# A graph network kernel: SyncE fetches the last chunk of some units row by row

## The chip, the cores and the metric

The kernel runs on one core of one Trainium2 chip. The core has five instruction streams: TensorE (PE, with its weight loads shown apart as PEld), VectorE (DVE), ScalarE (ACT), GpSimd (POOL) and SyncE (SP). SP computes nothing here: it issues transfers between HBM and the core's memory, one after the other in the order of the program. POOL issues the indirect transfers, whose row numbers come from a tile. The transfers of both run on the same 16 DMA engines.

The metric is the device time of one execution in microseconds, taken as the median of the runs.

## The reference

Four graph layers over 12,500 nodes of 128 features and 212,500 edges, which are sorted by their destination `dst`. Each layer takes a normalised and rectified copy of the node features, does something with the rows of each edge's source, and adds the result to the features:

```python
h = maximum(layernorm(x), 0); x = x + gat2(relu(gat1(h)))     # two graph attention convolutions
h = maximum(layernorm(x), 0); x = x + transformer(h)          # 8 heads, q of the node, k and v of the source
h = maximum(layernorm(x), 0); x = x + message_max(h)          # maximum over a node's edges, then an MLP
h = maximum(layernorm(x), 0)
sums = segment_sum(h[src], dst); x = x + sums / maximum(count(dst), 1)
```

All five edge steps (two in the first layer) need `table[src]`: for each edge one row of a table that was computed per node. This fetching of rows is what the change is about.

## The kernel before

**Tiles, chunks and units.** Nodes are handled in T = 98 tiles of P = 128. Edges are handled in 1661 chunks of 128, one edge to a partition. A unit `u` is U = 17 chunks in a row, which hold nearly all edges of node tile `u`; a tile also looks at the last 3 chunks of the unit before it and at the first 3 of the unit after it, 23 in all. The 17 chunks of a unit are fetched in 6 groups of GS = 3 chunks; the last group has only 2 (chunks 15 and 16).

**Preparation.** `prepared` (L413) derives from the edge lists what the passes need. `sd` holds all source numbers as float, edge after edge along each partition. `chunks(IDX, sd, ...)` (L470) transposes it on PE and DVE writes it as integers into `IDX`, where column k is chunk k. `ch` (L472) is a scratch tile of the same shape as `sd`.

**Five passes.** `edge_pass` (L1321) runs five times: `gat1` over the table `t1` (66 floats a row), `gat2` over `t2` (130), `attn` over `tkv` (264), `max` over `ts_` (128) and `sum` over `th` (129). The classes `gat`, `attn`, `maximum` and `total` say what each pass does with a chunk; `total` is the last one.

**Gathers.** `Pass.gather` (L1230) takes a tile `g` for a group from a ring of `bufs` buffers (18 groups in both gat passes, 17 in attn, 20 in max, 24 in sum) and has POOL issue one indirect transfer for each chunk (L1235): the column of `IDX` names 128 rows of the table, and each row lands in one partition. That makes 8305 gathers in the whole kernel, 1661 a pass.

**Use of a group.** `e1` is the first work on a group. In the gat passes it copies a logit out of `g` on ACT (L1523), in attn it multiplies by the queries on DVE (L1641), in max it transposes `g` on PE (L1701), in sum it does nothing but note where the chunk lies. Later `batch` (L1263) multiplies one-hot matrices (`se`, loaded at L1252, turned into float at L1281 on ACT) with the chunks on PE (L1290) and so sums the edges of a node tile into `acc` in PSUM, four chunks at a time. `ends` (L1294) loads `gt` (L1297, rows for tiles that don't fit the window), copies `acc` to `r` on ACT (L1311), lets DVE pick between `r` and `gt` (L1305) and hands `r` to the pass's own last step. In the sum pass that step is `after_sum`: three small DVE operations up to `o` (L932) and the store of the result by SP (L934).

**Order.** The order of all instructions is written out by hand. `edge_pass` keeps a calendar of rounds, RU = 24 to a unit; each piece of work is a generator that starts in a given round and goes one step further in each round. Within a round, pieces go by rank, lower first. `gather(u, i)` stands in round 24u - 24 + 4i, one unit ahead of `e1(u, i)` in round 24u + 4i. Each engine then works through its own instructions strictly in this order, and so does SP: a store that waits for its data holds up every transfer behind it. SP's transfers take turns over eight semaphores, so each also waits for the eighth before it to land.

Of the kernel before, what the change touches and what calls it, by code (L numbers as in the profile page):

```python
# [65 lines left out]
def gnn_kernel(ctx, tc, a, out):  # L66
# [18 lines left out]
    ww_d = dram.tile([3, D], BF16, name="ww_d")  # L85
    feat_d = dram.tile([T, 5, EW], BF16, name="feat_d")
    last_d = dram.tile([T, 5, EW], BF16, name="last_d")
    ewf_d = dram.tile([3, CP * P], BF16, name="ewf_d")
    first_d = dram.tile([1, (CP + 16) * P], BF16, name="first_d")
    xd = dram.tile([NP, D], F32, name="xd")  # L90
# [194 lines left out]
    def chunks(out, x, on):  # L285

        o = out.rearrange("p (r b) -> p r b", b=RC)
        for b0 in range(0, RC, 4):
            n = min(4, RC - b0)
            px = psum([P, 4, P], "b", "px")  # L290
            for b in range(n):
                PE.transpose(px[:, b, :], x[:, (b0 + b) * P:(b0 + b + 1) * P], ident)
            yield
            on(o[:, :, b0:b0 + n].rearrange("p r b -> p b r"), px[:, :n, :])
# [118 lines left out]
    def prepared(wp):  # L413
        tn_i = wp.tile([P, 1], I32, name="tn_i")
        GP.iota(tn_i, pattern=[[0, 1]], base=0, channel_multiplier=P)
        tid = wp.tile([T, 1], I32, name="tid")
        GP.iota(tid, pattern=[[0, 1]], base=0, channel_multiplier=1)
        tn = wp.tile([P, 1], F32, name="tn")
        V.tensor_copy(tn, tn_i)
        tn1 = wp.tile([P, 1], F32, name="tn1")  # L420
        V.tensor_scalar_mul(tn1, tn, -1.0)
        tn2 = wp.tile([P, 1], F32, name="tn2")
        V.tensor_scalar_add(tn2, tn, float(P))
        yield

        w = rd_[:, 1:EW + 1]
        eq = wp.tile([T, EW - P], BF16, name="eq")  # L430
        long_ = wp.tile([T, 1], F32, name="long_")
        V.scalar_tensor_tensor(eq, w[:, P:], 0.0, w[:, :EW - P], op0=ALU.add, op1=ALU.is_equal,
                               accum_out=long_)
        yield
        f = wp.tile([T, 2], F32, name="f")
        V.tensor_scalar(f[:, 0:1], rd_[:, 0:1], tn[:T, :], long_, op0=ALU.is_ge, op1=ALU.max)
        V.tensor_scalar(f[:, 1:2], rd_[:, EW + 1:], tn2[:T, :], f[:, 0:1], op0=ALU.is_lt,
                        op1=ALU.max)
        V.tensor_scalar_min(f[:, 1:2], f[:, 1:2], 1.0)
        yield  # L440
        p2 = psum([P, P], "mm", "p2")
        PE.transpose(p2[:1, :T], f[:, 1:2], ident[:T, :T])
        yield
        flag = wp.tile([1, T], F32, name="flag")
        V.tensor_copy(flag, p2[:1, :T])
        zr = wp.tile([1, T], F32, name="zr")
        V.memset(zr, 0.0)
        ord_ = wp.tile([1, T], F32, name="ord_")
        V.tensor_tensor_scan(ord_, flag, zr, 0.0, op0=ALU.add, op1=ALU.add)
        V.tensor_copy(NOV, ord_[:, T - 1:T])  # L450

        at = wp.tile([1, T], F32, name="at")
        V.scalar_tensor_tensor(at, flag, -float(2 * T), ord_, op0=ALU.mult, op1=ALU.add)
        V.tensor_scalar_add(at, at, float(2 * T - 1))
        yield
        pfl = psum([P, P], "mm", "pfl")
        PE.matmul(pfl[:, :T], ones[0:1, :], flag, start=True, stop=True)
        p3 = psum([P, P], "mm", "p3")
        PE.transpose(p3[:T, 0:1], at, ident[0:1, 0:1])
        yield  # L460
        V.tensor_copy(FLAG, pfl[:, :T])
        at_i = wp.tile([T, 1], I32, name="at_i")
        V.tensor_copy(at_i, p3[:T, 0:1])
        GP.indirect_dma_start(out=list_d, in_=tid, in_offset=None,
                              out_offset=bass.IndirectOffsetOnAxis(ap=at_i[:, 0:1], axis=0),
                              bounds_check=T - 1, oob_is_err=False)
        SY.dma_start(LIST, list_d.rearrange("(p t) c -> p (t c)", p=1))
        yield

        yield from chunks(IDX, sd, V.tensor_copy)  # L470

        ch = wp.tile([P, RC * P], F32, name="ch")  # L472
        V.tensor_tensor(ch, dd[:, 1:], dd[:, :RC * P], ALU.not_equal)
        yield
        yield from chunks(FIRST, ch, S.copy)
        m = wp.tile([P, RC * P], BF16, name="m")
        S.mul(m, ch, -BIG)
        SY.dma_start(first_d[0, P:(CP + 1) * P].rearrange("(p f) -> p f", p=P), m)
        yield
        dl = w  # L480
        V.tensor_scalar(dl, w, tn1[:T, :], FAR, op0=ALU.add, op1=ALU.min)
        V.tensor_scalar_max(dl, dl, -1.0)
        yield
        xb = wp.tile([T, EW], BF16, name="xb")
        S.copy(xb, dl)
        SY.dma_start(feat_d[:, 2, :], xb)
        hi, lo = yield from square(wp, dl, [T, EW], "q")
        for k, y in ((3, hi), (4, lo)):
            SY.dma_start(feat_d[:, k, :], y)
        yield  # L490
# [700 lines left out]
    def zero_rows(pool):  # L1191
# [3 lines left out]
        for _ in zeroed(gen_d, z, 7):  # L1195
            for _ in range(2 * RU):
                yield

    class Pass:


# [10 lines left out]

        made, whole = True, True

        def __init__(self):
            self.rhs, self.gs, self.f, self.fa, self.x, self.n0 = {}, {}, {}, {}, {}, {}
            self.st, self.se, self.acc = {}, {}, {}

# [6 lines left out]
        def x_load(self, t):  # L1225
            if self.source is not None:
                self.x[t] = features(self.source, t, self.width)
            yield

        def gather(self, u, i):  # L1230
            c, n = groups_of(u)[i]
            g = self.pool.tile([P, GS, self.wid], self.dt, name="g", bufs=self.bufs)
            for j in range(n):
                k = u * U + c + j
                GP.indirect_dma_start(  # L1235
                    out=g[:, j, :], out_offset=None, in_=self.table,
                    in_offset=bass.IndirectOffsetOnAxis(ap=IDX[:, k:k + 1], axis=0))
            self.gs[u, i] = g
            yield
# [81 lines left out]
    def edge_pass(name, table, wid, dt, wids, work_of, post, extra=()):  # L1321
        nonlocal ps_now
        w = work_of
        with tc.tile_pool(name=name, bufs=2) as pool, \
                tc.tile_pool(name="ps_" + name, bufs=1, space=PSUM) as pp, tc.manual_schedule():
            ps_now, w.pool, w.table, w.wid, w.dt, w.wids = (pp, w.banks), pool, table, wid, dt, wids
            cal = {}

            def at(r, rank, g):
                cal.setdefault(r, []).append((rank, g))  # L1330

            for u in range(T):
                r0 = u * RU
                at(r0 - RU, 0, w.load(u))
                at(r0 + RU - 4 - w.tail[0] * (u == T - 1), 0, w.load2(u))
                for i, _ in enumerate(groups_of(u)):
                    at(r0 - RU + i * RG, 0, w.gather(u, i))
                    at(r0 + i * RG, 5, w.e1(u, i))
                    if w.e2_at is not None:
                        e2_at = w.e2_at if u < T - 2 else w.e2_last or w.e2_at  # L1340
                        at(r0 + e2_at[i] - w.tail[0] * (u == T - 1), 4, w.e2(u, i))
                if w.chain_at is not None:
                    at(r0 + w.chain_at - w.tail[0] * (u == T - 1), 3, w.chain(u))
                n = len(w.batches(u))
                rt = r0 + w.tile_at
                loads = rt - RU
                rt -= w.tail[1] * (u == T - 2) + w.tail[2] * (u == T - 1)
                at(min(loads, rt + RU - 9 - 3 * (n - 1) - 2), 0, w.tile_load(u))
                at(rt, 0, w.x_load(u))
                for b in range(n):  # L1350
                    at(rt + RU - 9 - 3 * (n - 1 - b), 2, w.batch(u, b, n))
                at(rt + RU - 4, 1, w.ends(u, post))
            for g in extra:
                at(0, 1, g(pool))
            live, r = [], min(cal)
            while live or cal:
                live += cal.pop(r, [])
                live.sort(key=lambda g: g[0])
                live = [g for g in live if next(g[1], live) is not live]
                r += 1  # L1360
# [116 lines left out]
        V.tensor_tensor(c, x, b, ALU.subtract)  # L1477

    class gat(Pass):
        chain_at, e2_at, tile_at = RU + 5, range(RU + 13, 2 * RU + 1, 2), 2 * RU  # L1480

        def __init__(self, c, source=None):
# [116 lines left out]
            return r  # L1599

    class attn(Pass):
        bufs, source, width = 17, x2d, 2 * D
        chain_at, tile_at = RU + 7, 2 * RU + 2
        e2_at = [RU + 15 + r for r in (0, 2, 4, 6, 7, 11)]
# [68 lines left out]
            return r  # L1673

    class maximum(Pass):
        feats, bufs, source, made = last_d, 20, xd, False
        tile_at, tail = 12, (0, 0, 8)
        banks = {"pm": 1, "x": 2, "acc": 1, "pg": 2, "mm": 2}
# [45 lines left out]
            return r  # L1724

    class total(maximum):
        bufs, made = 24, True
        tile_at, tail = 10, (0, 0, 0)
        banks = {"acc": 2, "mm": 2}
# [173 lines left out]
```

## Time and profile before

| what | value |
|---|---|
| median of 3 runs | 10796.18 us (10791.58 to 10797.74) |
| the profiled execution, its own time | 10805.76 us |
| its span, first to last instruction | 10804.1 us |
| mean granted TensorE clock | 0.721 |
| gathers, first to last, gat1 | 159.7 to 2276.5 us |
| gat2 | 2319.9 to 4401.5 us |
| attn | 4441.5 to 6563.1 us |
| max | 6619.2 to 8694.3 us |
| sum | 8718.3 to 10797.0 us |

The busy share of each engine over the span, in 40 slices of 270 us (a digit is tenths; PEclk is the clock that TensorE was granted, DMA the share of the 16 transfer engines):

```profile
PE   3676666656556556677777777888888866666666
DVE  4555555544444444577777774333333310000000
ACT  4666666644444444355555554444344421111111
POOL 3777777767777777677777776777777767777777
PEclk6555555556676676799999998898888865555555
DMA  4332222224444444455555553333333323333333
```

The five passes can be told apart by the steps in these rows: gat1 up to the ninth digit, gat2 up to the sixteenth or seventeenth, attn to the twenty-fourth, max to the thirty-second, sum to the end. POOL's row hardly changes from pass to pass; the other engines' rows do.

### The profile page before, as it was taken

The numbers are of one execution on the slowest core, as the hardware profiler recorded it, in microseconds if no ns is written. First come the engines' busy times: TensorE is split into PE (matmuls) and PEld (weight loads), VectorE is DVE, ScalarE is ACT, GpSimd is POOL, SyncE is SP. The second block draws the span as 40 slices with busy tenths as digits, with TensorE's granted clock in tenths as the row PEclk, the third lists the DMA queues.
The fourth block names the chain that finished last, engine by engine and source line by source line (L and its number), as shares of the span: only waits on it lengthen the run. The fifth ranks groups of instructions, "written<-read, shape, count | busy, mean of one in ns | idle before, by whom it ended". The sixth has DMA issues, their size and how long they took to land. (4 is left out here: it accounts for less than half of the span.)

```text
span 10804.1 us, 149842 instructions
## 1 busy us (share of the span) xinstructions
PE 7525.6 (70%) x47184; PEld 5611.8 (52%) x47185; DVE 4565.5 (42%) x15188; ACT 4673.1 (43%) x13171; POOL 7928.6 (73%) x8330
## 2 busy tenths in 40 slices
PE   3676666656556556677777777888888866666666
PEld 2333333334444444566666666666666644444444
DVE  4555555544444444577777774333333310000000
ACT  4666666644444444355555554444344421111111
POOL 3777777767777777677777776777777767777777
PEclk6555555556676676799999998898888865555555
DMA  4332222224444444455555553333333323333333
GB/s 127 86 85 74 74 72 73 74 79 118 117 114 117 117 115 117 129 164 167 163 167 162 166 163 102 96 96 96 93 96 96 93 77 81 80 80 81 81 79 78
DMA packets 759391, 1146.93 MB, mean 106 GB/s; under 512 B 224152, under 2 KB 491623, under 8 KB 758479
## 3 DMA queue, kind: packets, MB, share of 16 engines
q0 software_dynamic: 292368, 610.29, 22.7%
q1 hardware_dynamic: 465536, 526.83, 15.0%
q8 instruction: 374, 6.13, 0.2%
q14 instruction: 441, 3.61, 0.1%
q10 hardware_dynamic: 672, 0.07, 0.0%
HBM read 964.76 MB, written 171.69 MB: 105 GB/s over the span
## 5 line engine op out<-in xcount | busy, mean ns | idle before, releaser
L1235 POOL DMA_INDIRECT g<-t,IDX x3322 | 3158.5, 951 | 1171.1 <-issue 692.6
L1290 PE MATMUL acc<-xf,sef 128*128 128x131 f32 (+2 forms) x13458 | 2292.1, 321 | 571.5 <-ACT sef L1281 545.2
L1290 PEld LDWEIGHTS acc<-xf,sef 128*128 128x128 f32 x13458 | 1985.4, 223 | 745.6 <-ACT sef L1281 609.0
L1235 POOL DMA_INDIRECT g<-tkv,IDX x1661 | 1615.8, 973 | 545.8 <-issue 407.4
L1235 POOL DMA_INDIRECT g<-ts__84,IDX x1661 | 1569.4, 945 | 561.8 <-issue 359.5
L1235 POOL DMA_INDIRECT g<-th,IDX x1661 | 1573.0, 947 | 529.6 <-issue 406.0
L1290 PE MATMUL acc<-g,sef 128*128 128x129 f32 x4486 | 1365.3, 445 | 722.2 <-DMA g<-th,IDX 613.2
L1290 PEld LDWEIGHTS acc<-g,sef 128*128 128x128 f32 x4486 | 999.2, 302 | 1088.4 <-DMA g<-th,IDX 732.4
L1281 ACT CAST sef<-se 128x512 f32<-128x512 fp8e4 (+1 forms) x1755 | 1028.6, 598 | 435.7 <-PE acc L1290 430.6
L1305 DVE COPY_PREDICATED r<-FLAG,gt 128x129 f32<-128x129 int32 (+2 forms) x490 | 145.5, 297 | 2139.0 <-ACT r L1311 2077.1
L1706 DVE TENSOR_TENSOR_SCAN fm<-n,fm,pg 128x384 f32<-128x384 bf16 (+1 forms) x585 | 566.3, 968 | 932.8 <-PE pg L1703 931.5
L1518 PE MATMUL ex<-ADX,st 128*128 128x6 bf16 x4486 | 354.4, 174 | 830.3 <-ACT st L1124 373.3
L1518 PEld LDWEIGHTS <-st 128*128 128x128 fp8e4 x4486 | 329.4, 113 | 1000.2 <-ACT st L1124 565.0
L1523 ACT COPY lg<-g 128x3 f32<-128x3 f32 (+1 forms) x1172 | 226.5, 193 | 1150.1 <-DMA g<-t,IDX 1091.3
L1311 ACT COPY r<-acc 128x129 f32<-128x129 f32 (+2 forms) x392 | 105.8, 270 | 1311.9 <-PE acc L1290 1311.8
L1290 PE MATMUL acc<-xs,se 128*128 128x201 bf16 x2243 | 483.7, 368 | 231.2 <-ACT x L1576 120.0
L1716 ACT COPY xf<-pt_f 128x384 f32<-128x384 f32 x586 | 270.5, 462 | 864.8 <-PE pt_f L1712 859.5
L1139 PE MATMUL pm_se<-NF,fa 5*128 5x128 bf16 x4486 | 586.3, 266 | 0.0
L1441 DVE TENSOR_TENSOR_SCAN fw<-n,lt 17x384 f32<-17x384 bf16 (+1 forms) x294 | 303.3, 1032 | 542.3 <-PE lt L1453 542.3
L1124 ACT ACTIVATE st<-pm_st,ones 128x384 fp8e4<-128x384 f32 (+2 forms) x877 | 471.2, 537 | 120.6 <-PE pm_st L1131 120.6
L1636 PE MATMUL qe<-q,st 128*128 128x128 bf16 x6729 | 484.7, 223 | 25.7 <-DVE g L1641 18.4
L1712 PE MATMUL pt_f<-ident,fm 128*128 128x128 f32 x1661 | 340.7, 316 | 208.6 <-DVE xf L1715 142.7
(1099 smaller groups left out, 12341.0 us busy)
## 6 DMA issues: line engine op xcount, KB each, us to landing
se<-se_d SPq DMA_DIRECT2D x294, 368.0 KB
st<-st_d SPq DMA_DIRECT2D x196, 368.0 KB
g<-t,IDX POOLq DMA_INDIRECT x3322
n<-first_d SPq DMA_DIRECT2D x97, 544.0 KB
st_d<-st SPq DMA_DIRECT2D x98, 368.0 KB
se_d<-se SPq DMA_DIRECT2D x98, 368.0 KB
g<-tkv,IDX POOLq DMA_INDIRECT x1661
g<-ts__84,IDX POOLq DMA_INDIRECT x1661
```

What stands on the lines that cost most here:

```text
L1124: S.activation(out, pm[:, :out.shape[1], :], AF.Relu, scale=-1.0, bias=ones[:, 0:1], saturate=False)
L1139: PE.matmul(pm[:, j, :], f[:, (c + j) * P:(c + j + 1) * P], NF, start=True, stop=True)
L1235: GP.indirect_dma_start(out=g[:, j, :], out_offset=None, in_=self.table, in_offset=bass.IndirectOffsetOnAxis(ap=IDX[:, k:k + 1], axis=0))
L1281: S.copy(se, self.se[t][:, at, :])
L1290: PE.matmul(acc[:, :m], se[:, j, :], x[:, i, :], start=(b == 0 and j == 0), stop=(b == n - 1 and j == len(ws) - 1))
L1441: V.tensor_tensor_scan(fw[:, s0 * P:(s0 + n) * P], n0[:, s0 * P:(s0 + n) * P], lt[:r, :n, :].rearrange("p j e -> p (j e)"), fw[:, s0 * P - ...
L1518: PE.matmul(ex[:, 6 * k:6 * k + 6], st, ADX[:, t, :, :].rearrange("p s v -> p (s v)"), start=(first and c0 == 0), stop=(stop and c0 + n - ...
L1523: S.copy(lg[:, 0, 1 + c0:1 + c0 + n, :], self.gs[u, i][:, :n, c + 1:c + 2])
L1636: PE.matmul(qe[0][:, k - c0, :], st, self.q[t][:, s * D:(s + 1) * D], start=(first and s == 0), stop=(stop and s == 2))
L1706: V.tensor_tensor_scan(fm[:, :m, :].rearrange("p j e -> p (j e)"), self.n0[u][:, cols], pg, self.prev, op0=ALU.add, op1=ALU.max)
L1712: PE.transpose(pt[:, j, :], fm[:, j, :], ident)
L1716: S.copy(ft[:, :m, :D], pt[:, :m, :])
```

## The change

It has four parts.

1. The preparation writes the source numbers to HBM a second time, as integers in the order of the edges: DVE copies `sd` into `ch`, SP stores it to `src_x`. `ch` is allocated earlier for it and is written again later, as before.
2. `row_units` picks the units whose last chunk is to be fetched by SP: `by_row = 8` in `gat`, `attn` and `maximum`, that is units 7, 15, ... 95 (12 in each of the four passes); `by_row = 4` in `total`, units 3, 7, ... 95 (24).
3. `fetch_rows(u, span)` is a new piece of work with rank -1, ahead of all else in its rounds. Its 188 rounds (92 in the sum pass) end in round 24u + 12. SP loads the chunk's 128 row numbers into a tile of one partition; then, spread over these rounds, it loads 16 of them at a time into 16 registers and issues one transfer for each row, from `table[v]` to partition q of the tile `gx`. `gx` holds two chunks and has two buffers. That is 9216 rows in the whole kernel.
4. `gather` of such a unit's last group uses `gx` in place of `g`, and POOL fetches only its first chunk. All later work finds the chunk where it found it before.

```diff
+    src_x = dram.tile([CP * P, 1], I32, name="src_x")
...
+        ch = wp.tile([P, RC * P], F32, name="ch")
+        V.tensor_copy(ch.bitcast(I32), sd)
+        SY.dma_start(flat(src_x), ch.bitcast(I32))
+        yield
         yield from chunks(IDX, sd, V.tensor_copy)
 
-        ch = wp.tile([P, RC * P], F32, name="ch")
         V.tensor_tensor(ch, dd[:, 1:], dd[:, :RC * P], ALU.not_equal)
...
+    RR = 16
+    row_regs = [SY.alloc_register(f"row{i}") for i in range(RR)]
...
+        by_row = None
...
+        def row_units(self):
+            if self.by_row is None:
+                return [], 0
+            span = self.by_row * RU - 4
+            return [(u, RU // 2 - span) for u in range(T - 1) if u % self.by_row == self.by_row - 1
+                    and u * RU + RU // 2 - span >= -RU], span
+
+        def fetch_rows(self, u, span):
+            g = self.gx[u] = self.pool.tile([P, 2, self.wid], self.dt, name="gx", bufs=2)
+            rw = self.pool.tile([1, P], I32, name="rw", bufs=2)
+            e0 = (u * U + U - 1) * P
+            SY.dma_start(rw, src_x[e0:e0 + P, :].rearrange("(o f) c -> o (f c)", o=1))
+            for r in range(4):
+                yield
+            q = 0
+            for r in range(span - 4):
+                while q < P and q * (span - 4) < (r + 1) * P:
+                    if q % RR == 0:
+                        SY.load(row_regs, rw[0:1, q:q + RR])
+                    v = SY.snap(row_regs[q % RR], min_val=0, max_val=NP - 1)
+                    SY.dma_start(g[q:q + 1, 1, :], self.table[ds(v, 1), :])
+                    q += 1
+                yield
+
         def gather(self, u, i):
             c, n = groups_of(u)[i]
-            g = self.pool.tile([P, GS, self.wid], self.dt, name="g", bufs=self.bufs)
+            by_row = i == NG - 1 and u in self.gx
+            if by_row:
+                g, n = self.gx.pop(u), n - 1
+            else:
+                g = self.pool.tile([P, GS, self.wid], self.dt, name="g", bufs=self.bufs)
             for j in range(n):
                 k = u * U + c + j
                 GP.indirect_dma_start(
...
+            units, span = w.row_units()
+            for u, r in units:
+                at(u * RU + r, -1, w.fetch_rows(u, span))
...
     class gat(Pass):
+        by_row = 8
     class attn(Pass):
+        by_row = 8
     class maximum(Pass):
+        by_row = 8
     class total(maximum):
+        by_row = 4
```

More of the change, by code (lines that the diff above doesn't have):

```diff
@@ L1213, in gnn_kernel @@
         made, whole = True, True
+        by_row = None
         def __init__(self):
+            self.gx = {}
             self.rhs, self.gs, self.f, self.fa, self.x, self.n0 = {}, {}, {}, {}, {}, {}
```

## The prediction

> **What bounds the kernel now.** I read the share of busy time first, then the costliest groups, then the gathers pass by pass.
>
> ```profile
> PE 7525.6 (70%) x47184; PEld 5611.8 (52%) x47185; DVE 4565.5 (42%) x15188; ACT 4673.1 (43%) x13171; POOL 7928.6 (73%) x8330
> L1235 POOL DMA_INDIRECT g<-t,IDX x3322 | 3158.5, 951 | 1171.1 <-issue 692.6
> L1235 POOL DMA_INDIRECT g<-tkv,IDX x1661 | 1615.8, 973 | 545.8 <-issue 407.4
> L1235 POOL DMA_INDIRECT g<-ts__84,IDX x1661 | 1569.4, 945 | 561.8 <-issue 359.5
> L1235 POOL DMA_INDIRECT g<-th,IDX x1661 | 1573.0, 947 | 529.6 <-issue 406.0
> ```
>
> POOL is busy for only 73%, but the 27% is mostly a gap of its own making: 0.30 us after every gather. The gathers alone, in a window around each pass (start:end, length, busy time and count, then clock, DMA share, GB/s):
>
> ```profile
> 159.00:2277.00 2118.00, 1582.64 (x1661) 0.50 0.30 77
> 2319.00:4402.00 2083.00, 1575.91 (x1661) 0.69 0.40 116
> 4441.00:6564.00 2123.00, 1615.81 (x1661) 0.96 0.56 164
> 6619.00:8695.00 2076.00, 1569.40 (x1661) 0.89 0.33 95
> 8718.00:10804.00 2086.00, 1573.03 (x1661) 0.57 0.31 80
> ```
>
> Length by 1661 gives 1.275, 1.254, 1.278, 1.250 and 1.256 us for a gather, in five passes with quite different clocks and other work. So POOL's rate of issue sets the length of all five. A unit of 17 gathers lasts 17 x 1.25 = 21.25 us. The timeline in the last pass shows it, and SP beside it:
>
> ```profile
> 9618.22 0.95 POOL L1235 DMA_INDIRECT g<-th,IDX  x1 [0.30 <-issue]
> 9619.21 0.31 DVE L1305 COPY_PREDICATED r<-FLAG,gt 128x129 f32<-128x129 int32 x1 [21.30 <-ACT r L1311]
> 9619.47 0.94 POOL L1235 DMA_INDIRECT g<-th,IDX  x1 [0.30 <-DMA g<-th,IDX]
> 9620.32 0.34 SPq L934 DMA_DIRECT2D out_x<-o  x1
> 9620.70 0.43 SPq L727 DMA_DIRECT2D x<-xd  x1
> 9621.23 0.38 SPq L1252 DMA_DIRECT2D se<-se_d  x1
> 9621.65 0.43 SPq L1297 DMA_DIRECT2D gt<-gen_d  x1
> 9640.46 0.34 SPq L934 DMA_DIRECT2D out_x<-o  x1
> ```
>
> Gathers start 1.25 us apart; SP issues four transfers in 1.8 us and then stands at the next store. SP's own waits say the same (total, times, longest):
>
> ```profile
> SPq L934 <- DVE o L932: 1898.8, 98, 27.5
> ```
>
> So 1899 of the last pass's 2086 us of SP are free, and the change spends them.
>
> **What goes.** Units 7, 15, ... 95 (12 of them) lose one gather in each of the first four passes, units 3, 7, ... 95 (24) in the last: 72 of 8305. At 1.25 us, and 1.278 in the attention pass, that is 60 x 1.25 + 12 x 1.278 = 90.3 us, all of it on the path. The two-chunk tile gx adds waits on POOL: in the changed order its gather names eight SP transfer semaphores, but they are those of the rows written to that buffer two row units before, and the sequencer passes such waits while the gather before still runs (every gap is 0.30 us, with such a wait or without). Nothing.
>
> **What comes, on SP.** 9216 rows. In the changed order each is a register operation and a one-row transfer; 16 rows share one load of registers. Rows of before that are nearest:
>
> ```profile
> L958 SPq TENSOR_LOAD <-NOV x4: 271/274/453, 169.3 to 171.6; - x4
> L958 SPq FUSED_REGOPS  x4: 147/147/159, 169.8 to 171.9; - x4
> L467 SPq DMA_DIRECT2D LIST<-list_d x1: 246/246/246, 73.0 to 73.0; - x1
> L603 SPq DMA_DIRECT2D wwr<-in_L_gnn_Wm x1: 291/291/291, 43.0 to 43.0; - x1
> ```
>
> Between two SP instructions lie 0.04 to 0.05 us (9620.66 to 9620.70). So a row, c, costs 0.147 + 0.045 + 0.246 + 0.045 = 0.48 us, and with the slower of each 0.159 + 0.05 + 0.291 + 0.05 = 0.55. No row of before has its address from a register. From below c can't be under 0.45 (0.147, 0.09 and the cheapest store of one row, 0.21); from above the issue of a 128-row load, 0.43, gives 0.72 with 0.16 and two gaps of 0.065. I take 0.52: the mean of 0.48 and 0.55, since a one-row transfer is what it is nearest to; 0.45 and 0.72 stay as ends.
>
> [...]
>
> *Last pass.* In four units POOL now needs 67 x 1.25 = 83.75 us (85 before). SP needs 128 c for rows, 8 x 0.32 = 2.6 for register loads, 2.3 for fetching the indices and waiting for them to land (0.29 and about 2: bounded by 0 and the 3.6 us that the chain of waits shows for a whole gather), and 4 x 1.8 = 7.2 for its transfers of before. With c = 0.52: 66.6 + 12.1 = 78.7. It fits, with 5 us to spare; it is full at c = (83.75 - 12.1)/128 = 0.56. Queued behind rows now are gt (L1297), x and se: some 32 rows, 17 us, push gt from 19 us before its use (9621.65 to 9640) to about 2.6 us before the store, and it has to land within that. If it is 2 us late each unit, DVE and then the store behind it wait, and SP loses 8 us in four units: full at 0.50. I take no loss, as DVE has 21 us idle there and the sums' banks are freed by ACT, not by DVE.
>
> *Other passes.* Eight units are 169 us; SP needs 66.6 + 4.9 + 8 x 12 issues x 0.45 = 115. It is full only at c = 0.94. The last row goes out 9 of a unit's 24 rounds (8 us) before the group's first use, against some 0.5 + 3 us for issue and landing; gather buffers for 17 groups or more take up a slip of a few us before POOL sees it. The cover that hides the rows is SP's free time; gone, each us of SP is a us of the pass.
>
> *Preparation.* DVE copies 128x1664 once more (1.8 us, as L473, 1.87) and a later write of ch waits for its store: 2 us, between 0 and 5.
>
> **Sum.** -90.3 + 2 = -88.3. The profiled execution took 10805.76 us (span 10804.1), 9.6 over the median of the runs shown, 10796.18. So 10717.5 for it and 10708 for the median.
>
> **Rivals.**
> 1. *SP bounds the last pass* (the slower side). From c = 0.56 each four units last 128 c + 12.1, so against before 24 x (128 c + 12.1 - 85) - 58.3: nothing at c = 0.589, over 0.2% slower from 0.596; 10954 us at 0.64, 11200 at 0.72. For it: a new kind of address, and a margin of 0.04 us. Against: four priced parts that all lie below.
> 2. *Rows or gt land too late in passes 1 to 3*, where a group's buffer is held nearly three units: compute slips, POOL waits for a buffer, and the 36 saved gathers come back, 45.3 us: 10753. Against: 8 us of room.
> 3. *Gathers get dearer*, as they share the transfer engines with 9216 rows (the attention pass, at a share of 0.56, has 1.278 for 1.250): 0.005 us each is 41 us, 10749. Against: rows of 0.3 to 1 KB add 9216 packets to 759391.
>
> **How the numbers follow.** A measurement tells 0.2% (21.6 us) from no change. Forecast, 10700 to 10735: 0.55. Rivals 2 and 3, or c of 0.56 to 0.58: 0.12, still faster. Near nothing (c about 0.58 to 0.596): 0.08. Rival 1 beyond: 0.25. So faster 0.67, same 0.08, slower 0.25. The range goes from 10698 (no loss in preparation, and the runs' spread) up to c = 0.62, 10890; beyond lie some 0.15. The likeliest's own range is 10700 to 10735.
>
> **What would show it.** Right: 8233 gathers still 1.25 us apart, SP rows spaced 0.5 to 0.55 us, the last pass's gathers over in about 2049 us, SP still waiting at L934's store. Wrong: rows 0.6 us apart or more, no wait at that store, POOL waiting for PE in the last pass; or a gather gap over 0.30 elsewhere.

## The result

| kernel | median (lowest to highest) | against the kernel before |
|---|---|---|
| before, run beside it | 10797.74 us (10791.58 to 10802.74) | |
| changed | 10915.97 us (10912.67 to 10918.39) | 1.0109 [1.0098, 1.012] |

The change costs 118 us, where a gain of 88 was forecast. Its profiled execution has a span of 10916.7 us, 112.6 more than the one before, at the same mean clock of 0.72.

From the page of the changed kernel, its shares of busy time and POOL's groups of gathers (busy us, mean ns of one, then the idle time ahead of them and what ended most of it):

```profile
PE 7564.5 (69%) x47184; PEld 5666.0 (52%) x47185; DVE 4567.8 (42%) x15189; ACT 4651.3 (43%) x13171; POOL 7854.9 (72%) x8258
L1277 POOL DMA_INDIRECT g<-t,IDX x3274 | 3124.2, 954 | 1179.4 <-issue 647.8
L1277 POOL DMA_INDIRECT g<-tkv,IDX x1637 | 1578.6, 964 | 696.0 <-issue 394.7
L1277 POOL DMA_INDIRECT g<-ts__85,IDX x1637 | 1546.2, 945 | 577.8 <-issue 362.1
L1277 POOL DMA_INDIRECT g<-th,IDX x1613 | 1525.8, 946 | 518.6 <-issue 400.5
```

A gather costs POOL about what it did (954, 964, 945 and 946 ns for 951, 973, 945 and 947), and POOL has 72 instructions and 73.7 us of work fewer. What grew most is one idle time: ahead of the gathers from `tkv`, the attention pass's table, 696.0 us where it was 545.8. The windows around the gathers of each pass of the changed kernel (start:end, length, POOL's busy time and count, granted clock, DMA share, GB/s) give the rest:

```profile
162.00:2280.00 2118.00, 1575.13 (x1649) 0.50 0.29 77
2332.00:4407.00 2075.00, 1571.68 (x1649) 0.70 0.41 116
4447.00:6696.00 2249.00, 1589.92 (x1649) 0.93 0.53 154
6774.00:8835.00 2061.00, 1557.59 (x1649) 0.89 0.33 96
8861.00:10910.00 2049.00, 1548.45 (x1637) 0.57 0.31 82
```

With first starts and last ends to a tenth of a us, and the gap to the next pass's first gather beside them, the 112.6 us fall into place:

| stretch | its gathers, before | after | gap behind it, before | after | change | forecast |
|---|---|---|---|---|---|---|
| up to the first gather | | | 159.7 | 162.2 | +2.5 | +2 |
| gat1 | 2116.8 | 2117.5 | 43.4 | 52.4 | +9.7 | -15 |
| gat2 | 2081.6 | 2074.1 | 40.0 | 40.8 | -6.7 | -15 |
| attn | 2121.6 | 2248.7 | 56.1 | 79.1 | +150.1 | -15.3 |
| max | 2075.1 | 2059.9 | 24.0 | 27.1 | -12.1 | -15 |
| sum | 2078.7 | 2047.3 | 7.1 | 7.6 | -30.9 | -30 |

The last two passes do what was forecast. The attention pass is 165 us off, gat1 25, gat2 8, max 3.

**Where the attention pass lost it.** The waits of VectorE for `gt`, the small table that it picks from, from 4440 to 6700 us of both kernels, before and after (total us, times, longest):

```profile
DVE r L1305 <- DMA gt<-gen_d: 5.7, 7, 1.5
```

```profile
DVE r L1347 <- DMA gt<-gen_d: 121.0, 91, 3.4
```

and the waits of POOL for the multiplication that frees a gather buffer, which before were only its usual gap of 0.3 us:

```profile
POOL g L1235 <- DVE xf L1665: 8.5, 28, 0.3
```

```profile
POOL g L1277 <- DVE xf L1712: 188.8, 110, 7.2
```

So VectorE waits in nearly every unit for `gt`, by 1.3 us; it reaches `e2` later, and POOL stands at a full ring of 17 groups. Why `gt` is late is seen in the timelines of one unit, first before, then after (start, duration, engine, line, operation):

```profile
5508.49 0.32 SPq L879 DMA_DIRECT2D xd<-u  x1
5508.86 0.74 SPq L1405 DMA_DIRECT2D n<-first_d  x1
5509.64 0.45 SPq L1297 DMA_DIRECT2D gt<-gen_d  x1
...
5513.02 0.31 DVE L1305 COPY_PREDICATED r<-FLAG,gt 128x136 f32<-128x136 int32 x1
...
5529.44 0.32 SPq L879 DMA_DIRECT2D xd<-u  x1
```

```profile
5535.26 0.35 SPq L884 DMA_DIRECT2D xd<-u  x1
...
5535.80 0.65 SPq L1264 DMA_DIRECT2D gx<-tkv  x2
5536.50 0.76 SPq L1450 DMA_DIRECT2D n<-first_d  x1
5537.50 0.26 SPq L1264 DMA_DIRECT2D gx<-tkv  x1
5537.81 0.37 SPq L1339 DMA_DIRECT2D gt<-gen_d  x1
...
5540.65 0.31 DVE L1347 COPY_PREDICATED r<-FLAG,gt 128x136 f32<-128x136 int32 x1 [0.78 <-DMA gt<-gen_d]
...
5557.05 0.35 SPq L884 DMA_DIRECT2D xd<-u  x1
```

SP stands at the store of `u` of tile t-1 until VectorE has made it. Only then does it come to `gt` of tile t; in the changed kernel rows have queued up between the two. And the next store needs what follows from that `gt`: from the pick through `after_attn`'s products, two normalisations and the MLP to `u` of tile t. That closes a loop: store, `gt`, pick, chain, store. Its mean over some 90 units of the pass, from the starts of those rows:

| from, to | before | changed |
|---|---|---|
| store of tile t-1, issue of `gt` of tile t | 1.16 us | 3.23 us |
| issue of `gt`, pick | 3.42 | 2.71 |
| pick, store of tile t | 17.17 | 17.44 |
| once around | 21.75 | 23.38 |

Before, the pick found `gt` already there in 91 of 98 units, and POOL's 17 gathers set the pace: in this pass they take 21.7 us (17 times 1.278), not 21.25, as 61 of its gathers were busy for over 1.1 us, while none had more than the usual gap ahead of it. Now `gt` sets the pace, and each unit is 1.6 us longer.

### The profile page after: what moved, and what is told of

The parts are those of the page before. It is cut to its first block, busy times and chain, and to the rows that moved or that the text cites. A ratio compares the mean times of both kernels' runs of the same rounds, so it can differ in the third digit from the quotient of the medians.

```text
span 10916.7 us, 178387 instructions
## 1 busy us (share of the span) xinstructions
PE 7564.5 (69%) x47184; PEld 5666.0 (52%) x47185; DVE 4567.8 (42%) x15189; ACT 4651.3 (43%) x13171; POOL 7854.9 (72%) x8258
## 5 line engine op out<-in xcount | busy, mean ns | idle before, releaser
L1277 POOL DMA_INDIRECT g<-t,IDX x3274 | 3124.2, 954 | 1179.4 <-issue 647.8
L1332 PE MATMUL acc<-xf,sef 128*128 128x131 f32 (+2 forms) x13458 | 2348.0, 327 | 590.1 <-ACT sef L1323 562.4
L1332 PEld LDWEIGHTS acc<-xf,sef 128*128 128x128 f32 x13458 | 2031.7, 228 | 775.2 <-ACT sef L1323 639.8
L1277 POOL DMA_INDIRECT g<-tkv,IDX x1637 | 1578.6, 964 | 696.0 <-issue 394.7
L1277 POOL DMA_INDIRECT g<-ts__85,IDX x1637 | 1546.2, 945 | 577.8 <-issue 362.1
L1277 POOL DMA_INDIRECT g<-th,IDX x1613 | 1525.8, 946 | 518.6 <-issue 400.5
L1332 PE MATMUL acc<-g,sef 128*128 128x129 f32 x4294 | 1303.3, 444 | 695.9 <-DMA g<-th,IDX 588.9
L1332 PEld LDWEIGHTS acc<-g,sef 128*128 128x128 f32 x4294 | 956.7, 303 | 1040.2 <-DMA g<-th,IDX 704.2
L1683 PE MATMUL qe<-q,st 128*128 128x128 bf16 x6729 | 509.9, 229 | 24.1 <-DVE g L1688 16.7
```

Source lines behind the costliest of these rows:

```text
L1277: GP.indirect_dma_start(out=g[:, j, :], out_offset=None, in_=self.table, in_offset=bass.IndirectOffsetOnAxis(ap=IDX[:, k:k + 1], axis=0))
L1332: PE.matmul(acc[:, :m], se[:, j, :], x[:, i, :], start=(b == 0 and j == 0), stop=(b == n - 1 and j == len(ws) - 1))
L1683: PE.matmul(qe[0][:, k - c0, :], st, self.q[t][:, s * D:(s + 1) * D], start=(first and s == 0), stop=(stop and s == 2))
```

## The experiments

**1. Cut the loop: `gt` ahead of the store.** The changed kernel with each tile's `gt` issued next to its `x` in all passes; in the attention pass that is some 17 us earlier (19.66 us from issue to pick).

```diff
     def x_load(self, t):
         if self.source is not None:
             self.x[t] = features(self.source, t, self.width)
+        gt = self.gts[t] = self.pool.tile([P, XW], F32, name="gt")
+        SY.dma_start(gt[:, :self.wids], gen_of(self.wids)[rows(t), :self.wids])
         yield
...
     def ends(self, t, post):
         acc = self.acc.pop(t)
-        gt = self.pool.tile([P, XW], F32, name="gt")
-        SY.dma_start(gt[:, :self.wids], gen_of(self.wids)[rows(t), :self.wids])
-        self.gt = gt
+        self.gt = self.gts.pop(t)
```

> The change kept whole, but each tile's gt load is issued beside its x load, some 10 us earlier in SP's order and ahead of the store at which SP stands, in all five passes. Theory G (gt is late for VectorE): the wait of copy_predicated for gt in the attention pass goes from 121.0 us to under 15, its gathers take about 2106 us (2121.6 less 12 gathers) for 2248.7, and the turn to the next pass is back from 79.1 to about 56 us: some 165 us less, 10750 us. Rival Q (the whole burst behind the store is late, gt is only the first that shows): another load of that burst (st, q, n) takes over as what is waited for, the gain stays under 60 us, 10860 or more. Rival M (the rows' traffic itself slows gathers or engines): no gain over 20 us, 10895 or more.

10746.05 us, 0.9955 [0.9939, 0.9972]. In the attention pass no wait of VectorE for `gt` is left; POOL's wait for `xf` and the window of the pass's gathers are

```profile
POOL g L1280 <- DVE xf L1713: 21.0, 69, 0.3
```

```profile
4447.00:6549.00 2102.00, 1597.99 (x1649) 0.96 0.58 166
```

2100.2 us to the tenth, 21.4 less than before, and 60.3 in the gap behind it. The 69 waits are 0.3 us each, the gap that POOL has after any gather. All rows are still fetched in that pass, so neither their traffic nor the lateness of the loads behind `gt` costs what was lost. That is theory G, and it is all of the attention pass but some 4 us of the gap.

**2. The control: `gt` moved in the kernel before**, the same edit without any rows.

> The kernel before with gt issued beside x, no rows. It is the control for gt_early. Theory L: before, the loop (1.16 + 2.75 + 17.2 = 21.1 us) lies just under POOL's 17 gathers (21.25), so cutting it gains little: 5.7 us of waits for gt in the attention pass and 11 in the first, 10785 to 10797 us. If moving gt is itself worth what gt_early gained, 10740 to 10760.

10797.73 us, 0.9996 [0.9986, 1.0005]; the attention pass's gathers take 2121.8 us for 2121.6. Moving `gt` alone is worth nothing: it gives back what the rows had taken.

**3. Make the delay without the rows.** The first try put a register load, whose registers nothing read, ahead of `gt` in the kernel before.

```diff
     def ends(self, t, post):
...
+        for i in range(self.late):
+            SY.load(row_regs, IDX[0:1, 0:16])
         SY.dma_start(gt[:, :self.wids], gen_of(self.wids)[rows(t), :self.wids])
```

> The kernel before, with no row fetched; in the attention pass alone a load of 16 registers (1.23 us in the changed kernel) stands in SP's queue ahead of each gt. Theory G: gt comes 1.28 us later, the 98 units lose 100 to 130 us between them and the turn some 20, 10900 to 10950 us, with VectorE waiting for gt in nearly every unit and POOL waiting for the products that free its buffers. Rival Q expects a loss too, as the loads behind gt are late as well; gt_early tells these apart. Rival M: no row is moved, so within 20 us of before, 10800 to 10820.

10794.69 us, 0.9999 [0.9989, 1.0008], which says nothing of the theories: the profile has no register load on that line, and `gt` follows `n` as it did before. That load, which no one uses, isn't in the program that ran. The run only shows how closely no change is measured.

The second try keeps the load alive: one row, addressed by a register, goes into an unused tile.

```diff
+        if self.late:
+            SY.load(row_regs, IDX[0:1, 0:16])
+            v = SY.snap(row_regs[15], min_val=0, max_val=NP - 1)
+            jk = self.pool.tile([1, self.wid], self.dt, name="jk")
+            SY.dma_start(jk, self.table[ds(v, 1), :])
         SY.dma_start(gt[:, :self.wids], gen_of(self.wids)[rows(t), :self.wids])
...
     class attn(Pass):
+        late = True
```

> The kernel before, gathers and all; in the attention pass alone one register load of 16, whose last register addresses one row that is fetched into an unused tile, stands ahead of each gt. It is what gt_delay was to be, in a form that the program keeps. Theory L (a loop through SP's queue: the store of tile t-1, gt of tile t, copy_predicated, the chain of VectorE, the store of tile t): store to gt goes from 1.16 to about 2.8 us, gt to its use stays at some 2.75 (where it is waited for) and use to next store at 17.4, so a unit lasts 22.95 us for 21.75 and the pass some 115 us longer, with 20 in the turn: 10930 us. Rival M (the traffic of the 128-row fetches): one row per unit is 1/16 of it, 10795 to 10815.

10890.88 us, 1.0086 [1.0069, 1.0102]. The waits of VectorE and of POOL in the attention pass:

```profile
DVE r L1313 <- DMA gt<-gen_d: 76.3, 95, 3.2
```

```profile
POOL g L1238 <- DVE xf L1674: 98.5, 82, 2.9
```

One row a unit, and all 1661 gathers kept, bring 62 us in the gathers (2183.5) and 24 in the gap (79.7): the same two waits, the same place. Rival M is out. The loop measures 3.27 + 2.11 + 17.26 = 22.64 us. The size was expected too high: store to `gt` grew by more than assumed (the register load took 1.48 us at the median here), but `gt` then lands in 2.11 us, not in the 2.71 that it takes with the rows of the full change about.

**4. Undo the attention part, and do it alone.**

```diff
     class attn(Pass):
-        by_row = 8
+        by_row = None
```

> The change without its attention part (no unit is fetched by rows there). Theory G, and Q: the attention pass is back at 2121.6 us and the turn behind it at 56, some 150 us less than the changed kernel, 10765 us, so faster than before by some 0.3%. Rival M, with a slowdown in all passes: the loss is spread and at most 60 us come back, 10855 or more.

10757.89 us, 0.9964 [0.9951, 0.9976]: the other four passes' parts together are a gain of 37 us. In its profiled execution (10786.63 us) the attention pass's gathers take 2131.5 us, with 59.2 behind them, and VectorE waits 5.6 us for `gt` in 9 times.

> The attention part of the change alone; the other four passes fetch nothing by rows. Theory G and Q: the whole loss is in this pass, +127 us in its gathers and +23 in the turn, 10945 us. If the rows of the passes before and behind it feed the loss (buffers or a lag handed over), less: under 10890.

10967.86 us, 1.0159 [1.0142, 1.0176], 173 us lost where 150 were expected; in its trace 149.3 us lie in the pass's gathers (2270.9) and 21.8 in the gap (77.9). Within the full change the two are 150; what makes the 21 us between them was not looked into.

**5. gat1.** Its loss lies in two places: POOL's five waits in the first 310 us, at the start of the pass, are 41.5 us in place of 29.8, and the gap behind the pass is 9.0 longer, as the other engines end later: the last store of `t` goes out 49.1 us after the pass's last gather, 40.2 before. From the starts of the picks of units 7 and 28, a unit took 20.51 us before, 20.95 in the changed kernel and 21.13 in experiment 1. POOL's 17 gathers take 21.25: POOL had run ahead here, and the other engines, which start late behind the preparation (before, the first pick comes 121.8 us after the first gather in gat1, 27 to 68 in the other passes), are catching up. So POOL didn't set the pace of this stretch.

```diff
     def __init__(self, c, source=None):
         super().__init__()
         self.c, self.w, self.source, self.made = c, c + 3, source, source is not None
+        if not self.made:
+            self.by_row = None
```

> gt_early without rows in the first GAT pass. In gt_early that pass and the turn behind it last 2173.2 us, against 2160.2 before, although POOL issues 12 gathers fewer: units 0 to 28 take 21.1 us for 20.5, in a stretch that POOL doesn't set. If SP's rows delay that stretch's loads, they go back to 20.5 and the pass to 2160: 10733 us. If POOL did set it, 12 more gathers cost 15 us: 10761 us.

10735.25 us, 0.9938 [0.9921, 0.9954]. The units are back at 20.50 us, POOL's early waits at 29.8, and pass and gap at 2157.8: SP's rows in gat1 cost what was lost there. (So it is without `gt` moved: with no rows in gat1, the attention part alone has 2159.8.) By which load or wait is not shown. In the changed kernel VectorE waits for `gt` in this pass too:

```profile
DVE r L1347 <- DMA gt<-gen_d: 76.4, 49, 10.9
```

where before had 11.2 us in 4 times. But in experiment 1 that wait is gone, and pass and gap are no shorter (2173.2 us, 2169.9 in the changed kernel). TensorE has a new wait there,

```profile
PE pm_se L1144 <- ACT st L1129: 60.8, 91, 0.7
```

0.67 us in each of 91 units, which neither the kernel before, the changed kernel nor no_gat1 shows. This matmul waits for ScalarE there, and for a semaphore of VectorE in the kernel before and the changed one (96 times in each). What made it so, and whether it alone kept the pass long, was not settled; the kernel of experiment 6 has it too, in 63 units.

**6. What the findings allow.** Experiment 1 with rows in gat1 only from unit 39 on, and one unit of four in the maximum's pass.

```diff
+        row_from = 0
...
-            return [(u, RU // 2 - span) for u in range(T - 1) if u % self.by_row == self.by_row - 1
+            return [(u, RU // 2 - span) for u in range(self.row_from, T - 1) if u % self.by_row == self.by_row - 1
                     and u * RU + RU // 2 - span >= -RU], span
...
     class gat(Pass):
...
+            if not self.made:
+                self.row_from = 39
...
     class maximum(Pass):
-        by_row = 8
+        by_row = 4
```

> gt_early with rows in the first GAT pass only from unit 39 on (8 units), where POOL sets the pace, and one unit of four for one of eight in the maximum's pass (12 gathers fewer). If the first pass's loss lies in its first 30 units, that pass and its turn take 2150 us (23 less than gt_early); if SP has room in the maximum's pass (it waits 851 us of 2060 at its stores, and 12 more units of rows cost some 780), 15 less there: 10708 us. If SP's queue fills up in the maximum's pass, its gathers take more than 2060 us and the whole is over 10725.

10710.04 us, 0.9919 [0.9902, 0.9935], the fastest of all, 91 us under before. Pass and gap of gat1 take 2149.0 us, for 2150 expected. The windows around the gathers of each pass:

```profile
163.00:2268.00 2105.00, 1574.40 (x1653) 0.50 0.34 78
2312.00:4385.00 2073.00, 1569.62 (x1649) 0.71 0.44 116
4424.00:6529.00 2105.00, 1601.22 (x1649) 0.96 0.58 166
6583.00:8629.00 2046.00, 1545.72 (x1637) 0.89 0.36 97
8652.00:10698.00 2046.00, 1545.97 (x1637) 0.56 0.35 82
```

In the maximum's pass 24 gathers fewer than before are 30.4 us fewer (2044.7 for 2075.1), and SP is all but full: its wait at that pass's store, 851.4 us in the changed kernel, is down to

```profile
SPq L922 <- DVE st L708: 60.5, 18, 17.3
```

## Why the prediction was wrong, step by step

**POOL's rate of issue bounds the passes: right in max and sum, half right in gat2.** A gather still starts 1.249 to 1.251 us after the one before (median of every pass), and 12 fewer in max and 24 fewer in sum shortened their gathers by 15.2 and 31.4 us. In gat2 12 fewer brought 7.5: 28 steps from gather to gather were over 1.5 us, for 11 before. POOL didn't wait in them (no idle time there is over 0.32 us); the gathers themselves took longer, as told under rival 3. "All of it on the path" was wrong for gat1: 1.275 us for a gather there was read as POOL's rate, while the mean hid 29.8 us in five early waits of POOL, and 28 units at 20.5 us that other engines set.

**The cost of a row: right in sum, wrong in its parts.** From the trace of the changed kernel, SP's register loads, its register operations and, for the sum pass alone, its rows (min/median/max ns, first and last start):

```profile
L1262 SPq TENSOR_LOAD <-rw x576: 983/1231/1872, 165.6 to 10852.3; - x192
L1263 SPq FUSED_REGOPS  x9216: 44/44/56, 166.7 to 10862.6; - x197
L1264 SPq DMA_DIRECT2D gx<-th x3072: 224/228/293, 8865.4 to 10862.8; - x192
```

The register operation takes 44 ns (147 were taken), the row 228 (246), and 16 registers take 1231 ns, where the 274 of a single one had been taken. The errors nearly cancel, and that is luck:

```profile
9708.85 15.01 SPq L1264 DMA_DIRECT2D gx<-th  x29
```

is 29 rows with two register loads among them, 0.518 us each; taken were 0.52 and 0.02 for the load. Without a load between, a row starts 0.42 us after the one before (median of all passes), so c was under the 0.45 that the prediction took as its lowest.

**The last pass fits, and the late `gt` costs nothing there: right.** SP still waits at its store,

```profile
SPq L939 <- DVE o L937: 252.6, 98, 19.4
```

10.5 us in four units, twice the 5 that were forecast: rows and register loads together were cheaper than taken. VectorE waits 110.7 us for `gt` in that pass (5 times, 35.5 the longest) and the pass isn't longer for it. So rival 1 did not come.

**Preparation: +2.5 for +2.**

**"Gather buffers for 17 groups or more take up a slip of a few us before POOL sees it": this step failed.** The prediction put the cost of late rows and loads in the first four passes at nothing. That treats lateness as a slip that happens once and that buffers hide. But the attention pass has a loop through SP's own queue, and a delay inside a loop comes back in every unit: 2.07 us more ahead of `gt`, less some 0.7 that the loop had to spare, and with 0.27 more in the chain, are 1.6 us in each unit, and a ring of buffers only puts off the first of them: POOL's first wait over its usual gap comes after 304 gathers of that pass, 385 us in. The room of SP was counted over eight units (115 of 169 us), and it was there, as SP's wait at that store in the changed kernel's attention pass shows:

```profile
SPq L884 <- DVE st L708: 960.3, 93, 13.6
```

What mattered was the order within 1.2 us of one wait. The prediction worked out the push on `gt` for the last pass, where `gt` went out 19 us before its use, and not for the pass where it had 0.7 to spare.

**Rival 2 had the mechanism, with the wrong price.** "Rows or gt land too late in passes 1 to 3 ... POOL waits for a buffer" is what happened, in attn. Its price was capped at "the 36 saved gathers come back, 45.3 us", as if a pass could at worst be as long as before. It has no such cap: attn alone gave back its 15.3 and 150 more. Experiments 1 and 3 show both directions of it.

**Rival 3, dearer gathers, came in gat2 alone, as far as is seen:** a gather there takes 0.953 us for 0.949, some 7 us over the pass, which is what it fell short by. The five kernels with rows in gat2 have 0.952 to 0.955, the five without 0.947 to 0.950; why was not looked into. In attn it is 0.964 (0.973 before), in the last two passes 0.945 and 0.946 (0.945 and 0.947).

## What to carry to other kernels

A queue that is idle for much of the time (here SP, for 960 of 2249 us at one store) is not always free for new work: look at what stands right behind its longest wait, how long after that wait its consumer needs it, and whether the consumer leads back to the same wait. If it does, anything put in between that exceeds what the loop has to spare is paid once per turn of the loop, not once (here 1.6 us in each unit); neither mean room nor 17 groups of buffers absorbed it, and moving the one needed load ahead of the wait brought the pass's gathers from 2248.7 to 2100.2 us. And test a pass's bound by stretches: a mean per pass can mix a stretch that another engine sets with one that the bound sets (gat1: 1.275 us a gather over the pass, while its units 7 to 28 took 20.51 us for the 21.25 of 17 gathers).

## What was not expected of the hardware

- A load of 16 registers took 1231 ns at the median (1478 from another tile, in experiment 3), one of a single register 274 in the kernel before (four of them). A register operation of 44 ns stands beside four of 147 to 168 in the same program.
- SP issues a one-row transfer with an address from a register in 228 ns, less than the 246 to 291 of the one-row transfers with fixed addresses that were taken as its nearest rows.
- Where it was waited for, `gt` took a mean of 2.71 us from issue to use with the one-row transfers of the whole change about, and 2.11 with a single one ahead of it; why was not looked into.
